# Moving the next batch's image sums, spectra and attention weights forward within layer 0

## The chip, the cores and the metric

The kernel runs on one core of a Trainium2 chip. The metric is the device time of one execution in microseconds (us). Before the change it is 3184.69 us, the median of three runs (3173.39 to 3188.97). Nothing else runs on the chip's other cores.

## The reference

The input `x` has shape (4, 32, 128, 128) in fp32: 4 batches of T = 32 images, each with 128 rows (w) and 128 columns (c). Two layers follow one another, each added to its input.

Layer 0 first normalizes `x` over groups of four columns and then runs an attention among the 32 images of a batch, built from Fourier layers. Cut to what matters here:

```
xa = group_norm(x)                       # per batch
xn = inorm(xa)                           # per image: mean and variance
k, q, v = fno(xn, K), fno(xn, Q), fno(xn, V)     # 32 heads each; k, q at half size
p_attn = softmax(q . k / 64)             # 32 x 32 weights for each head
p = fno(p_attn . v, P)                   # back to one channel
a = inorm(p + xa);  an = inorm(a)
m = gelu(inorm(spectral(an, m0)) + skip)
m = inorm(spectral(m, m1)) + skip
x = x + (inorm(m) + a)
```

`fno` is a spectral convolution (64 x 33 modes of the two-dimensional Fourier transform, with weights) and a scalar skip. Layer 1 is a causal additive attention over 4096 tokens of 128 columns in each batch, and a mixture of eight experts, the best two taken for each token.

## The kernel before

**Layer 1** (from L1022 on) takes some two thirds of the time. It starts when layer 0 ends, apart from a first piece that runs inside layer 0's last batch. The change does not touch it.

**Layer 0** (`layer0`, from L109 on) loops over the 4 batches (L687). The scores of the attention can be formed in Fourier space from spectra of the input images, and so can the values' product; the big tensors k, q and v are never made. One pass of the loop does, in this order of the program:

1. *Value product* (L698 to L788). The image spectra `xd` are read back from DRAM, spread over partitions (`xb`, DMAs of L758, four buffers), copied to PSUM by ScalarE (`xw`, L767), multiplied with the weights `gb` by VectorE (L775) or GpSimd (L773) to `u`, and multiplied with the attention probabilities `pr` on TensorE (L778, `po`). ScalarE puts the sums into `rs` (L788). The skip part `q` is made beside it (`skips`, L719), from `cp`, `cd` and `bd` (L703 to L711).
2. *Value inverse* (L792 to L815). `py` (L798) rearranges `rs` into `yf`; `inverse` (L267) brings each image back in two matmuls (`pv2`, L273, and `four`, L278), and `add_p` (L809) adds it to `q` and takes its statistics (`bn_stats`, L813).
3. *First transform* (L831 to L934). `stats` (L216) gives mean and variance of `q`; `spectra(0, q)` (L852) takes the forward transform: `first_step` (L243) makes `pz`, evacuated to `z1`, and L871 makes `px`; L873 to L891 multiply with the weights (`part1`, `part2`, `spec`) and square. `weighed` (L894) turns the squares into the variance of the result by Parseval's rule: L899, L906, L909, L915, a matmul with ones (`ms`, L314) and a copy (L918). Small operations give the scales `hq`, `hs0` and `hb`.
4. *First per-image inverse* (L935 to L955). `back` (L288) brings the images back in two halves of 16, with matmuls `y1` (L297) and `four` (L308); `gelu` (L939) adds the skip on VectorE (L941), applies the gelu on ScalarE (L944) and takes statistics (L951). `add_attention` (L845) adds the attention part to the input tile (L848), for 16 images after each half.
5. *Next batch's image sums* (L959, `image_sums`, L320). Squares on ScalarE (L326), 16 matmuls that sum rows (L330), small matmuls (`s12`, `mg`, `bg`, `my`) and about 36 small VectorE operations give the group and image statistics, the scaled transform matrix `colg` and the scales `ysc`.
6. *Second transform* (L963 to L967), as the first, of the gelu's result `gl`.
7. *Next batch's image spectra* (L969, `spectra_of_images`, L418). Four groups of 8 images go through `forward` (L253): `pz` (L248), evacuated to `z`, a correction of the mean (L434, L435), `px` in two matmuls for each image (L263, L264), and a scaling to `xx` (L429). Each group's spectra go to DRAM (L445). Then ScalarE copies the lowest modes into `xm` (L457).
8. *Statistics of the second transform* (L970 to L992): `weighed` twice (`v1`, `vc`), two inverse roots (`inv_std`, L204), and the scales `c2`, `c3` and `cq`.
9. *Next batch's attention weights* (L994, `attention_weights`, L487). For each of 17 columns of modes, two products of 128x1024 are made, 22 by VectorE and 12 by GpSimd in all (`pa`, `pb`, L522 and L524, a ring of six buffers), and TensorE multiplies them with weights (`sp`, L528). Then follow the sum `sc`, a softmax (L558 to L564), and a way through DRAM (`prd`, L572, to `pr`, L577).
10. *Second per-image inverse* (L995 to L1016). ScalarE scales `gl` (L999), GpSimd adds it to the input tile `xr` (L1006, 8 images at a time), `back` brings the images back, and VectorE adds them (L1010). The result goes to DRAM as `x1` (L1016).

The program's order is not the order on the chip: a scheduler orders each engine's instructions by readiness in its own model of time and by their place in the program, an earlier place going first. Once the program is built, each engine executes its instructions in the order written. A tile that names a tag shares the buffers of that tag and waits until an older tile there is released. `evacuate` (L184) sends two of three copies out of PSUM to ScalarE and every third to VectorE.

Of the kernel before, what the change touches and what calls it, by code (L numbers as in the profile page):

```python
# [13 lines left out]
P = 128  # L14
# [94 lines left out]
def layer0(  # L109
# [74 lines left out]
    def evacuate(out, in_, sign=1.0):  # L184

        flip[0] = (flip[0] + 1) % 3
        if flip[0]:
            nc.scalar.activation(out, in_, AF.Copy, scale=sign)  # L188
        else:
            nc.vector.tensor_scalar(out, in_, sign, None, ALU.mult)  # L190
# [120 lines left out]
    def sums(name, matrix, src):  # L311

        m = ps.tile(list(src.shape), F32, name=name, tag="wide")
        nc.tensor.matmul(m, matrix, src, start=True, stop=True)  # L314
        return m
# [4 lines left out]
    def image_sums(b, xt):  # L320


        rows8 = ps.tile([64, 4, C], F32, name="rows8", tag="wide")
        for g in GROUPS:
            xx2 = grp.tile([P, GI, C], F32, name="xx2", tag="pr", bufs=6)
            nc.scalar.activation(xx2, xt[:, g : g + GI], AF.Square)  # L326
            for h in range(2):
                m = g // 4 + h
                for k, src in enumerate((xt[:, 4 * m : 4 * m + 4], xx2[:, 4 * h : 4 * h + 4])):
                    nc.tensor.matmul(  # L330
                        rows8[32 * k : 32 * k + 32],
                        one_of_8[:, 7 - m : 39 - m],
                        src,
                        start=m == 0,
                        stop=m == 7,
                    )
        ev = grp.tile([64, 4, C], F32, name="ev", tag="v", bufs=3)
        nc.scalar.copy(ev, rows8)
        s12 = ps.tile([P, 2, 512], F32, name="s12", tag="wide")[:, :, :T]
        for j in range(4):  # L340
            for k in range(2):
                r = slice(32 * k, 32 * k + 8)
                nc.tensor.matmul(s12[:, k, j::4], ev[r, j], ident[r, r], start=True, stop=True)
        sv = small.tile([P, 2, T], F32, name="sv", tag="pk_sq")
        nc.vector.tensor_copy(sv, s12)

        tot = one("tot", 2)
        nc.vector.tensor_reduce(tot, sv, AX.X, ALU.add)
        mg = sums("mg", group, tot)
        gm = one("gm")  # L350
        nc.vector.tensor_copy(gm, mg[:, 0:1])
        gv = one("gv")
        nc.vector.tensor_mul(gv, gm, gm)
        nc.vector.tensor_tensor(gv, mg[:, 1:2], gv, ALU.subtract)
        gr, _ = inv_std("gn_r", gv, 1)
        gs = one("gs")
        nc.vector.tensor_mul(gs, gm, gr)

        both = small.tile([P, 2, 32], F32, name="both", tag="both")
        nc.vector.tensor_scalar(both[:, 0], of_group, gr, None, ALU.mult)  # L360
        nc.vector.tensor_scalar(both[:, 1], of_group, gs, -1.0, ALU.mult, ALU.mult)
        by_group = small.tile([P, 2, 32], F32, name="by_group", tag="by_group")
        nc.vector.tensor_copy(by_group, sums("bg", ones, both))
        n = 1 + 2 * KY
        colg = small.tile([P, 2, n], F32, name="colg", tag="colg")
        nc.vector.tensor_scalar(colg[:, 0], cols1[:, :n], gr, None, ALU.mult)
        nc.vector.tensor_scalar(colg[:, 1], cols2[:, :n], gr, None, ALU.mult)
        m128 = one("m128")
        nc.vector.tensor_scalar(m128, gm, 128.0, None, ALU.mult)

        gs128 = one("gs128")
        nc.vector.tensor_scalar(gs128, gs, 128.0, None, ALU.mult)
        gg = one("gg")
        nc.vector.tensor_mul(gg, gs, gs128)
        gr2 = one("gr2")
        nc.vector.tensor_mul(gr2, gr, gr)
        grs = one("grs")
        nc.vector.tensor_scalar(grs, gs, gr, -2.0, ALU.mult, ALU.mult)
        y12 = small.tile([P, 2, T], F32, name="y12", tag="pk")
        nc.vector.tensor_scalar(y12[:, 0], sv[:, 0], gr, gs128, ALU.mult, ALU.subtract)  # L380
        nc.vector.tensor_scalar(y12[:, 1], sv[:, 1], gr2, gg, ALU.mult, ALU.add)
        nc.vector.scalar_tensor_tensor(
            y12[:, 1], sv[:, 0], grs, y12[:, 1], ALU.mult, ALU.add
        )
        nc.vector.tensor_scalar(y12, y12, 1.0 / NPIX, None, ALU.mult)
        my = sums("my", ones, y12)
        ym, yv = per_image("ym"), per_image("yv")
        nc.vector.tensor_copy(ym, my[:, 0])
        nc.vector.tensor_mul(yv, ym, ym)
        nc.vector.tensor_tensor(yv, my[:, 1], yv, ALU.subtract)  # L390
        yr, _ = inv_std("n1_r", yv)
        ysc = scalars(ALU.mult, "n1_s", yr, par[:, N1W : N1W + 1])
        return by_group, colg, m128, ysc
# [24 lines left out]
    def spectra_of_images(b, xt, normed):  # L418


        _, colg, m128, ysc = normed
        n = 1 + 2 * KY
        xx = modes.tile([P, T, n], F32, name=f"xx_{b}", tag="xx")
        xd = dram.tile([T, 2, KX, KY], F32, name=f"xd_{b}")
        for g in GROUPS:

            def scaled(k, px):
                i = slice(g + k, g + k + 4)
                nc.vector.tensor_tensor(  # L429
                    xx[:, i], px, ysc[:, i].unsqueeze(2).to_broadcast([P, 4, n]), ALU.mult  # L430
                )

            def less_mean(z):
                nc.vector.tensor_scalar(z[:, :, 0], z[:, :, 0], m128, None, ALU.subtract)  # L434
                nc.vector.tensor_scalar(z[:, :, P], z[:, :, P], m128, None, ALU.add)  # L435

            forward([xt[:, g + t] for t in range(GI)], colg[:, 0], colg[:, 1], scaled, less_mean)

            i = slice(g, g + GI)

            for r, y in ((0, 1 + KY), (64, 1)):
                bias = par[r : r + 1, N1B : N1B + 1].to_broadcast([1, GI])
                nc.vector.tensor_copy(xx[r : r + 1, i, y], bias)
            for part in range(2):
                nc.sync.dma_start(  # L445
                    out=xd[i, part].rearrange("t x y -> x t y"),
                    in_=xx[64 * part : 64 * part + 64, i, 1 + KY :],
                )


        nc.vector.tensor_copy(xx[32:33, :, 0], xx[32:33, :, 1 + KY + 32])
        nc.vector.memset(xx[96:97, :, 0], 0.0)


        xm = modes.tile([P, 2 * KA, T], F32, name=f"xm_{b}", tag="xm")
        for k, y0 in enumerate((1 + KY, 1)):
            nc.scalar.copy(  # L457
                xm[:, k * KA : (k + 1) * KA], xx[:, :, y0 : y0 + KA].rearrange("p t y -> p y t")
            )
        return xx, xm, xd  # L460

    def value_weights():
        t1, t2 = (prep.tile([NH, KX, KA], F32, name=f"v{n}", tag=f"t{n}") for n in (1, 2))
# [117 lines left out]

    value_weights()
    normed = image_sums(0, loaded)
    front = spectra_of_images(0, loaded, normed)


    shape = [P, KA, NH]
# [99 lines left out]
    for b in range(B):  # L687
# [105 lines left out]
        for y0 in range(0, KY, 8):  # L793
            n = min(8, KY - y0)
            py = ps.tile([P, 8, 2, T], F32, name="py", tag="b")
            for k in range(n):
                for part in range(2):
                    nc.tensor.matmul(  # L798
                        py[64 * part : 64 * part + 64, k],
                        rs[:, :, y0 + k],  # L800
                        comb[:, 32 * part : 32 * part + 64],
                        start=True,
                        stop=True,
                    )
            evacuate(yf[:, :, :, y0 : y0 + n].rearrange("p t r y -> p y r t"), py[:, :n])
        st = grp.tile([P, T, 6], F32, name="st", tag="st")
        for g in GROUPS:

# [123 lines left out]
        nc.vector.tensor_scalar(hb, hb, par[:, S0 : S0 + 1], None, ALU.mult)  # L932
        nc.vector.tensor_mul(dq, dq, hs0)
        nc.vector.tensor_tensor(hb, hb, dq, ALU.add)  # L934
        gl = big.tile([P, T, C], F32, name=f"g_{b}", tag="y")  # L935
        st = grp.tile([P, T, 6], F32, name="st", tag="st")
        for a in HALVES:
# [14 lines left out]

            back(spec, a, gelu)
            for g in (16 * a, 16 * a + GI):
                add_attention(g)  # L955

        logarithms()
        if b + 1 < B:
            normed = image_sums(b + 1, loaded)  # L959
        else:  # L960
            first((ps, images))

        glm, glv, flat = stats("gl", st)  # L963
# [2 lines left out]
        nc.vector.tensor_copy(dg, d1)  # L966
        spec, sq = spectra(1, gl)  # L967
        if b + 1 < B:
            front = spectra_of_images(b + 1, loaded, normed)  # L969
        v1 = weighed("v1", sq, squares, layers[1][2])  # L970
        vc = weighed("vc", sq, squares, layers[1][3])
        r1, _ = inv_std("r1", v1)
# [17 lines left out]
        nc.vector.tensor_scalar(cq, cq, par[:, MB : MB + 1], None, ALU.add)  # L990
        nc.vector.tensor_mul(dg, dg, c3)
        nc.vector.tensor_tensor(cq, cq, dg, ALU.add)  # L992
        if b + 1 < B:
            weights = attention_weights(b + 1, front)  # L994
        for a in HALVES:  # L995
            groups = [slice(16 * a + g, 16 * a + g + GI) for g in (0, GI)]
            for i in groups:
# [648 lines left out]
```

## Time and profile before

| what | value |
|---|---|
| median of three runs | 3184.69 us (3173.39 to 3188.97) |
| the profiled execution's own time | 3191.62 us |
| its span, first to last instruction | 3189.9 us |
| granted TensorE clock, mean | 0.953 of full |
| busy: TensorE, VectorE, ScalarE, GpSimd | 92%, 72%, 72%, 66% of the span |
| start of py in batches 0 to 3 | 181.6, 440.4, 708.0, 967.5 us |
| layer 0 ends at about | 1105 us |

The span is 1.7 us shorter than the profiled execution's time. In the profile PE is TensorE, PEld its weight loads, DVE VectorE, ACT ScalarE, POOL GpSimd, SP SyncE, whose queue issues most DMAs; ACTq is ScalarE's own issuing of DMAs. An fp32 matmul leaves two records, so that counts of PE instructions in the trace are twice those of the program. In a line of the timeline come the start, the time covered, engine, source line, operation, output<-input with shapes, count, and in brackets the idle time before it and what ended it. Time between two rows that overlap is shared: small operations can start before the one ahead has ended.

### The profile page before, as it was taken

The page shows a single profiled execution, that of the slowest core. Times are in us where ns is not written, and L with a number is a line of the kernel's source. Part 1 is how long each engine was busy: PE and PEld are TensorE (multiplying, and loading weights), DVE is VectorE, ACT ScalarE, POOL GpSimd, SP SyncE. Part 2 cuts the span into 40 slices and gives each one's busy share as a digit, 9 for nine tenths or more (in the row PEclk, how much of TensorE's full clock was granted, in tenths as well). Part 3 has the DMA queues.
Part 4 walks back from the last instruction along what each step waited for, and adds up shares of the span by engine and source line. Part 5 has one row for each costly group of instructions (what it writes and reads, how often), then busy time and mean ns, then how long its engine had stood idle before and what let it go on. Part 6 is the DMA issues. An engine that isn't in the chain of part 4 may idle for free.

```text
span 3189.9 us, 53099 instructions
## 1 busy us (share of the span) xinstructions
PE 2928.7 (92%) x19634; PEld 1438.2 (45%) x19634; DVE 2290.9 (72%) x5035; ACT 2311.7 (72%) x3138; POOL 2102.7 (66%) x1831
## 2 busy tenths in 40 slices
PE   7888798798888789999999999999999999999997
PEld 5366365345546444444344443444444444444443
DVE  5876666667677566777666868866778777687887
ACT  2344243253343589998999999998999999999992
POOL 1621540460451289878788797889878889888773
PEclk6998998899898799999999999999999999999998
DMA  6301310130140211010111010011010011101000
GB/s 140 111 18 30 95 50 3 49 123 1 30 130 2 57 31 31 8 31 7 31 37 24 14 24 14 8 39 31 23 29 9 14 37 24 37 1 31 14 14 14
DMA packets 152308, 112.77 MB, mean 35 GB/s; under 512 B 36878, under 2 KB 140657, under 8 KB 151441
## 3 DMA queue, kind: packets, MB, share of 16 engines
q1 hardware_dynamic: 136209, 103.61, 12.2%
q10 hardware_dynamic: 15840, 5.77, 0.8%
q8 instruction: 155, 2.54, 0.3%
q14 instruction: 104, 0.85, 0.1%
HBM read 68.37 MB, written 20.00 MB: 28 GB/s over the span
## 4 chain that ended last, share of the span: by engine, by line
PE 61%; POOL 12%; ACT 9%; DVE 9%; issue 7%; DMA 1%; ACTq 0%; POOLq 0%; DVEq 0%; SPq 0%
PE d L1446 19%; PE po L1465 11%; PE px L1352 6%; ACT r L1496 4%; PE po L778 4%; PE n L1446 3%; POOL e L1505 3%; POOL e L1504 3%; PE pz L248 2%; PE four L308 2%; ACT e L1512 2%; PE px L871 1%; PE sk L742 1%; POOL kx L1111 1%; DVE r L1501 1%
## 5 line engine op out<-in xcount | busy, mean ns | idle before, releaser
L1501 DVE TENSOR_TENSOR r<-n,r 128x1024 f32<-128x1024 f32 (+1 forms) x1056 | 961.6, 952 | 479.0 <-PE n L1446 389.4
L1504 POOL TENSOR_TENSOR e<-r 128x512 f32<-128x512 f32 x528 | 673.2, 1275 | 268.1 <-DVE r L1501 267.6
L1496 ACT ACTIVATE r<-d 128x1024 f32<-128x1024 f32 (+1 forms) x1056 | 792.9, 802 | 67.4 <-PE n L1446 56.4
L1508 ACT ACTIVATE r<-r 128x1536 f32<-128x1536 f32 x528 | 783.6, 1484 | 16.8
L1505 POOL TENSOR_TENSOR e<-e,r 128x512 f32<-128x512 f32 x528 | 671.3, 1271 | 41.4
L1446 PE MATMUL d<-qe,ke 32*128 32x512 f32 (+3 forms) x2304 | 605.8, 602 | 39.6 <-ACT r L1496 36.5
L1465 PE MATMUL po<-e,kx 128*128 128x512 f32 (+3 forms) x1152 | 594.5, 605 | 15.6 <-POOL e L1517 15.6
L1446 PE MATMUL n<-qe,ke 32*128 32x512 f32 (+3 forms) x2304 | 606.2, 601 | 0.0
L1446 PE MATMUL n<-qf,kf 32*128 32x512 f32 (+3 forms) x2304 | 552.6, 554 | 0.0
L1446 PE MATMUL d<-qf,kf 32*128 32x512 f32 (+3 forms) x2304 | 550.2, 553 | 0.0
L1356 DVE SCALAR_TENSOR_TENSOR xc<-px,wgt,xc 128x128 f32<-128x128 f32 x1024 | 358.1, 350 | 42.2 <-PE px L1352 9.7
L1512 ACT ACTIVATE e<-e 128x512 f32<-128x512 f32 x528 | 325.8, 617 | 66.2 <-POOL e L1505 65.6
L1465 PEld LDWEIGHTS po<-e,kx 128*128 128x128 f32 x1152 | 175.5, 188 | 392.8 <-issue 306.9
L1446 PEld LDWEIGHTS d<-qe,ke 32*128 32x128 f32 x2304 | 176.5, 183 | 359.3 <-ACT r L1496 339.5
L773 POOL TENSOR_TENSOR u<-xb,gb 128x858 f32<-128x858 f32 (+1 forms) x120 | 233.1, 1968 | 139.5 <-PE po L778 128.0
L1446 PEld LDWEIGHTS d<-qf,kf 32*128 32x128 f32 x2304 | 220.2, 186 | 176.1 <-issue 163.8
L1352 PE MATMUL px<-we,x2t 128*128 128x512 f32 x512 | 264.0, 601 | 6.8 <-DVE xc L1356 6.0
L775 DVE TENSOR_TENSOR u<-xw,gb 128x858 f32<-128x858 f32 (+1 forms) x200 | 206.6, 1082 | 59.2 <-PE po L778 46.6
L885 POOL TENSOR_TENSOR spec<-part,part 128x512 f32<-128x512 f32 x16 | 24.8, 1550 | 333.4 <-ACT z L188 75.2
L1446 PEld LDWEIGHTS n<-qf,kf 32*128 32x128 f32 x2304 | 228.3, 185 | 19.2 <-issue 11.4
L778 PE MATMUL po<-u,pr 128*32 128x429 f32 (+1 forms) x1280 | 191.1, 548 | 26.8 <-DVE u L775 11.7
L524 POOL TENSOR_TENSOR pb<-xm 128x1024 f32<-128x1024 f32 x48 | 90.7, 1913 | 159.1 <-ACT xm L457 152.8
(388 smaller groups left out, 3953.9 us busy)
## 6 DMA issues: line engine op xcount, KB each, us to landing
xb<-xd SPq DMA_DIRECT2D x128, 214.5 KB
xc<-x SPq DMA_DIRECT2D x29, 512.0 KB
x<-x SPq DMA_DIRECT2D x16, 512.0 KB
qf<-qe SPq DMA_DIRECT2D x64, 128.0 KB
out<-xc SPq DMA_DIRECT2D x15, 512.0 KB
xb<-xd SPq DMA_DIRECT2D x32, 198.0 KB
gb<-gd SPq DMA_DIRECT2D x4, 1056.0 KB
x<-in_x SPq DMA_DIRECT2D x8, 512.0 KB
```

The lines of the kernel that those rows point to most:

```text
L773: nc.gpsimd.tensor_tensor(u, xb, gk, ALU.mult)
L778: nc.tensor.matmul(po[32 * j : 32 * j + 32], pr[:, i, k], u[:, r], start=i == 0 and k == 0, stop=i == 3 and k == 1,)
L1352: nc.tensor.matmul(px, x2t[:, k * P : (k + 1) * P], we[:, e0 : e0 + 4], start=True, stop=True)
L1356: nc.vector.scalar_tensor_tensor(xc[:, k], px[:, e], wgt[:, k, e0 + e : e0 + e + 1], xc[:, k], ALU.mult, ALU.add)
L1446: nc.tensor.matmul(o, k, q, start=turn == 0 or g > 0, stop=turn == 1 or g > 0)
L1465: nc.tensor.matmul(sums[c, h][:, q0 : q0 + c1 - c0], kx[:, jb], e[:, c0:c1], start=jb == 0, stop=is_last and q0 > 2 * P, skip_group_check= ...
L1496: nc.scalar.activation(r[:, g], d, AF.Ln, scale=1.0 / DSCALE)
L1501: nc.vector.tensor_tensor(r[:, g], part, r[:, g], ALU.mult)
L1504: nc.gpsimd.tensor_tensor(e, r[:, 1], r[:, 2], ALU.add)
L1505: nc.gpsimd.tensor_tensor(e, e, r[:, 0], ALU.add)
L1508: nc.scalar.activation(r, r, AF.Exp, scale=-1.0)
L1512: nc.scalar.activation(e, e, AF.Exp)
```

## The change

The sums, spectra and weights of the next batch stay what they are and move to other places in the program:

- The image sums go from behind the gelu stage to between `py` and the value inverse (into step 2).
- The spectra become a generator. Its first yield hands out the tiles `xx`, `xm` and `xd`; each of the four groups of images is then one step. One step is taken ahead of the first per-image inverse, and one ahead of each group of 8 images of `add_attention`, so that two come between the two halves and the last one after the second half (into step 4). The fourth step runs to the end, with the copies to `xm`.
- The attention weights go from behind the statistics of the second transform to just behind `spectra(1, gl)`, ahead of `v1` and `vc` (between steps 6 and 8).
- `sv` gets a buffer of its own, where it shared one with `pk_sq` of `stats`; `y12`, which shared one with `pk`, is dropped, its operations being done in place on `sv`.

```diff
@@ image_sums
-        sv = small.tile([P, 2, T], F32, name="sv", tag="pk_sq")
+        sv = small.tile([P, 2, T], F32, name="sv", tag="sv")
...
-        y12 = small.tile([P, 2, T], F32, name="y12", tag="pk")
-        nc.vector.tensor_scalar(y12[:, 0], sv[:, 0], gr, gs128, ALU.mult, ALU.subtract)
-        nc.vector.tensor_scalar(y12[:, 1], sv[:, 1], gr2, gg, ALU.mult, ALU.add)
-        nc.vector.scalar_tensor_tensor(
-            y12[:, 1], sv[:, 0], grs, y12[:, 1], ALU.mult, ALU.add
-        )
-        nc.vector.tensor_scalar(y12, y12, 1.0 / NPIX, None, ALU.mult)
-        my = sums("my", ones, y12)
+        nc.vector.tensor_scalar(sv[:, 1], sv[:, 1], gr2, gg, ALU.mult, ALU.add)
+        nc.vector.scalar_tensor_tensor(sv[:, 1], sv[:, 0], grs, sv[:, 1], ALU.mult, ALU.add)
+        nc.vector.tensor_scalar(sv[:, 0], sv[:, 0], gr, gs128, ALU.mult, ALU.subtract)
+        nc.vector.tensor_scalar(sv, sv, 1.0 / NPIX, None, ALU.mult)
+        my = sums("my", ones, sv)
@@ spectra_of_images
         xd = dram.tile([T, 2, KX, KY], F32, name=f"xd_{b}")
+        xm = modes.tile([P, 2 * KA, T], F32, name=f"xm_{b}", tag="xm")
+        yield xx, xm, xd
         for g in GROUPS:
...
+            if g + GI < T:
+                yield
...
-        xm = modes.tile([P, 2 * KA, T], F32, name=f"xm_{b}", tag="xm")
...
-        return xx, xm, xd
@@ before the loop over batches
-    front = spectra_of_images(0, loaded, normed)
+    front, *_ = spectra_of_images(0, loaded, normed)
@@ behind py, ahead of the value inverse
+        if b + 1 < B:
+            normed = image_sums(b + 1, loaded)
         st = grp.tile([P, T, 6], F32, name="st", tag="st")
@@ ahead of the first per-image inverse
+        ahead = iter(())
+        if b + 1 < B:
+            ahead = spectra_of_images(b + 1, loaded, normed)
+            front = next(ahead)
+            next(ahead)
         gl = big.tile([P, T, C], F32, name=f"g_{b}", tag="y")
...
             back(spec, a, gelu)
             for g in (16 * a, 16 * a + GI):
+                next(ahead, None)
                 add_attention(g)

         logarithms()
-        if b + 1 < B:
-            normed = image_sums(b + 1, loaded)
-        else:
+        if b + 1 == B:
             first((ps, images))
...
         spec, sq = spectra(1, gl)
         if b + 1 < B:
-            front = spectra_of_images(b + 1, loaded, normed)
+            weights = attention_weights(b + 1, front)
         v1 = weighed("v1", sq, squares, layers[1][2])
...
         nc.vector.tensor_tensor(cq, cq, dg, ALU.add)
-        if b + 1 < B:
-            weights = attention_weights(b + 1, front)
         for a in HALVES:
```

## The prediction

> **What bounds the kernel now.** Layer 0 takes about 1105 of the span's 3189.9 us; the change stays inside its batches 0, 1 and 2, each of which prepares the next. I cut batch 0 into stages by events in the timeline (py starts, statistics of q, first gelu add, last gelu statistics, end of the second transform, sod, last product, next po) and asked for the busy time of each stage. Columns: stretch, its length, then busy time (instructions) of PE, PEld, DVE, ACT, POOL, then granted clock, DMA share, GB/s:
>
> ```profile
> 181.60:208.60 27.00, 25.55 (x290) 24.37 (x294) 15.10 (x46) 9.46 (x12) 0.00 (x0) 1.00 0.01 2
> 208.60:235.70 27.10, 20.35 (x219) 14.79 (x209) 23.27 (x88) 6.77 (x17) 3.44 (x2) 0.79 0.01 2
> 235.70:257.10 21.40, 19.47 (x114) 7.08 (x114) 16.71 (x66) 16.47 (x37) 0.00 (x0) 0.94 0.00 1
> 257.10:276.80 19.70, 19.58 (x191) 13.95 (x190) 10.00 (x53) 6.83 (x15) 1.26 (x1) 1.00 0.01 1
> 276.80:308.80 32.00, 28.38 (x232) 27.25 (x226) 20.40 (x72) 8.30 (x18) 1.26 (x1) 0.86 0.24 57
> 308.80:342.20 33.40, 24.31 (x130) 4.88 (x130) 26.85 (x23) 13.12 (x35) 31.73 (x16) 0.78 0.06 16
> 342.20:371.50 29.30, 20.44 (x165) 9.48 (x166) 17.37 (x46) 6.42 (x12) 4.17 (x3) 1.00 0.32 80
> ```
>
> Call them A (py, inverse), B (first transform, its statistics), C (gelu), D (image sums, second transform), E (image spectra), F (attention products), G (softmax, last inverse). In A and E the PE is the full engine. In B VectorE is: the PE timeline shows the hole.
>
> ```profile
> 220.50 1.74 PE L871 MATMUL px<-z,cst 128*32 128x256 f32 x24
> 228.57 0.63 PE L314 MATMUL ms<-v_s,ones 128*128 128x32 f32 x2 [6.34 <-DVE v_s L915]
> 229.13 4.14 PE L297 MATMUL y<-cst,spec 32*128 32x128 f32 x64
> ```
>
> F is bound by POOL, 31.7 of 33.4 us, which does more than products: the POOL timeline has the four adds of L1006 among them.
>
> ```profile
> 309.04 3.78 POOL L524 TENSOR_TENSOR pb<-xm 128x1024 f32<-128x1024 f32 x2 [28.68 <-ACT xm L457]
> 312.77 2.37 POOL L1006 TENSOR_TENSOR x<-x,g 128x1024 f32<-128x1024 f32 x1
> 315.83 2.37 POOL L1006 TENSOR_TENSOR x<-x,g 128x1024 f32<-128x1024 f32 x1 [0.69 <-ACT g L999]
> 318.15 3.79 POOL L524 TENSOR_TENSOR pb<-xm 128x1024 f32<-128x1024 f32 x2
> ```
>
> The scalings that feed these adds run under the products on ScalarE, and G ends on VectorE, where the cp reductions and the next batch's first u stand behind the last adds of L1010:
>
> ```profile
> 309.88 12.04 ACT L999 ACTIVATE g<-g,cq,c 128x128 f32<-128x128 f32 x31
> ...
> 365.29 2.16 DVE L1010 SCALAR_TENSOR_TENSOR x<-four,c,x 128x128 f32<-128x128 f32 x8 [0.25 <-PE four L308]
> 367.36 1.28 DVE L705 TENSOR_TENSOR cd<-cm,sel 128x512 f32<-128x512 f32 x2
> 368.56 1.91 DVE L706 TENSOR_REDUCE cp<-cd 128x16 f32<-128x512 f32 x2
> 370.38 1.04 DVE L775 TENSOR_TENSOR u<-xw,gb 128x858 f32<-128x858 f32 x1
> ```
>
> **What the Trainium skill says.** "TensorE: Matmul & The Clock Gate" (Part 1, the HAM clock gate) says an idle window of about 3.4 us halves the PE's clock. The trace agrees at the hole in B: after 6.34 us idle the clock is 0.50 until 235. It also halves after idles of only 1.5 us in E (0.50 from 300 to 315), so I can't promise a warm clock in C. The same page (opening table, queue depth) calls ScalarE, VectorE and GpSimd strict FIFO. The trace agrees: products of L524 wait behind L1006. This decides G below. "GPSIMD Engine Reference" (1. Specifications) says POOL shares its SBUF interface with VectorE instructions that have two SBUF inputs. In batch 1, L899 took 1.91 instead of 1.21 us beside L885; the durations I use contain such meetings already.
>
> **The change part by part.** From the instruction order of the built program, by stage; times are gains (-) or losses (+) per batch, for batch 0 first.
>
> A, image sums added. PE gets 16 matmuls of L330; x and xx run in pairs, 0.43 us per record pair, two of these per pair of matmuls. Three precede py, 13 follow it: 6.5 x 0.86 = 5.6 us, of which 1 us fills the wait for yf. The 36 small VectorE operations of the sums (0.13 to 0.2 us each) fall in a stretch where VectorE is full (in batch 1, 8 adds at 0.6, 32 statistics at 0.22 and three evacuations at 0.6 take 13.5 of the 14.5 us from the first q add on): about 30 x 0.13 = 3.9 us. The first q add comes 5.5 us later (rows, s12, mg), hence 5.5 + 3.9, less 0.7 of slack: **+8.7** (bounds +6, +11). Squares (L326) run before this already. The x loads they need are issued a whole batch earlier and land under the value products.
>
> B, group 0 of the spectra added. PE work (8 pz at 0.255, 16 px at 0.223: 5.6 us) lies in the hole and costs nothing; were the hole gone, it would be +5.6. VectorE, which bounds B, gets 2 evacuations (0.6), 2 mean corrections (0.2), 2 scalings (0.44) and 2 copies: **+3.1**.
>
> C, groups 1 and 2 added, between the two halves of the inverse. Half one: 16 adds at 0.26 and 16 statistics at 0.22, behind gelus at 0.39 with a table load of 1.3: 9 us. Then in PE's order the rest of y1 (3.1), 32 px (7.1), 10 pz (2.5) and their evacuations stand before half two's first inverse matmul; this starts about 19 us after the first add, and needs 8.6. Together 27.8 against 21.4: **+6.4**. With a half clock px takes 0.43: +7 more, the upper bound; the lower one is +3. In batch 1, C took 27.6 at a clock of 0.64: there +0.2.
>
> D loses the image sums and rows' tail, and gets group 3: px 3.6, then the second transform, whose evacuations on ScalarE now wait for xm (2.25) and a table load (1.3). I count 17.3 us against 19.7, 21.7 and 21.4: **-2.4**, -4.4, -4.1 (bounds +4, -6).
>
> E goes but for sod's matmuls, 1.3 us: **-30.7**, -30.1, -31.3. The xd writes (8 issues of 0.65 us on SP) and the xb loads behind them move ahead with it; SP is idle there, and po waits for VectorE's u, not for xb, so this gains nothing.
>
> F: POOL's order has the 12 products and then the four adds: 12 x 1.91 = 22.9 us. VectorE becomes the bound: sod 1.2 and 22 products, issued every 1.15 us, 26.5; PE at a half clock would need 17 x 1.7 = 29. I take 28: **-5.4**.
>
> G pays for it. VectorE's order puts v1 and vc of the second transform (L899, L906, about 1.2 us each, four) *behind* the 22 products, since the weights now come first, and all that follows from them is late: r1, rm, c2, cq, then 32 scalings on ScalarE, four adds on POOL, the last adds on VectorE. From the last product on: four reductions and softmax to 10.3 us; about 25 small operations and two inverse roots of 1.7 to cq at 15.1. The pr DMA, queued on ScalarE before the scalings, waits for prd until about 14.5, so it is not later. 16 scalings at 0.39 end at 21.4, the second add of 2.37 at 23.8; half two's 16 with three evacuations end at 29.3, its last add at 31.7. Then 12 last adds (3.3), an evacuation, cd, 4 adds (3.1), cp (1.9), u (1.0): po starts at 41 against 29.3, 30.6 and 27.3: **+11.7**, +10.4, +13.7. Bounds: +6 if the last adds overlap more, +18 if nothing does.
>
> Sums: -8.6 in batch 0, -17.6 in batch 1, -9.0 in batch 2, together -35.2. Batch 3 and layer 1 get the same instructions as before. The new sv tag takes the place of two shared ones; it ends no wait that the trace shows. The profiled execution took 3191.6 us, 1.7 more than its span and 0.2% over the median of 3184.7; the same step from the median gives **3150**.
>
> **Rivals.**
> 1. *As above*, 3112 to 3172, about 3150. For it: E is a stretch of 32 us with PE full, whose work fits into stages where PE or the other engines have room. Against: it must survive seven terms.
> 2. *Tail decides*: G's chain costs the full +18, and A the full +11; then a batch gains about 3 and the kernel takes about 3175 to 3185, near no change. For it: every link is on another in-order queue.
> 3. *Slower*: the spectra stand in series in C. PE executes in order, so half two of the gelu stage waits for 32 px matmuls whose evacuations stand behind the gelus on ScalarE. If nothing overlaps and the clock is half there, C takes 21.4 plus 32 px at 0.43 (13.8) and three rounds of evacuation, correction and scaling (about 2.5 each): +21 instead of +6.4, so that a batch loses about 3 on average and the time is about 3195 to 3205. It decides once C passes 40 us. Against: the gelu stage in batches 0 and 2 leaves ScalarE 5 and VectorE 5 us idle.
> 4. *More than thought*: the filled hole keeps the clock, C costs +2, and F runs at 26.5: 5 to 6 us more per batch, about 3132. That the change does nothing (the scheduler having hoisted this work already) is excluded: in the order before, sums and spectra stand behind the gelus.
>
> **Chances.** First 0.60, fourth 0.14, second 0.15, third 0.11. The range that leaves out 2 in 10 reaches from 3112 to 3186. A measurement of this kernel can tell about 0.5%, 16 us. Faster by more: cases one and four but for their edge, 0.74; within it: 0.15; slower: 0.11.
>
> **What would show it.** After: py to first q statistics about 36 us; no stretch like E; POOL's L1006 adds behind all twelve products; last product to next po about 41 us with ScalarE's scalings in it. Wrong if that last stretch stays near 30, or grows beyond 47, if C passes 40, or if F stays at 33 without the adds.

## The result, and the profile after

| | us |
|---|---|
| the changed kernel, median of 12 runs | 3197.9 (3186.0 to 3208.0) |
| the kernel before, 12 runs beside it | 3177.7 (3173.4 to 3189.0) |
| ratio, 95% interval | 1.0053 (1.0035 to 1.0072) |
| forecast | 3150 (3112 to 3186) |

The change makes the kernel slower by half a per cent, some 17 to 20 us, where I forecast 35 us faster. The profiled execution took 3204.4 us, its span 3202.7, at a mean clock of 0.948 (before: 0.953); it is 6.5 us above the median of the twelve. One execution of `e7_vahead` below, 4013.5 us at a mean clock of 0.66, is left out of that run's ratio.

The time is lost in the place that the prediction named, batches 0 to 2 of layer 0: from the first py to that of batch 3 it was 786 us and is 801. A second profile of each kernel (`before_again` and `after_again`, below) has 770 and 798. All stages below are cut as in the prediction. First batch 0 of the changed kernel, A to G, with the columns of before (length, then TensorE, its weight loads, VectorE, ScalarE, GpSimd, clock):

```profile
180.80:219.90 39.10, 37.02 (x336) 30.63 (x338) 19.30 (x80) 10.65 (x17) 0.00 (x0) 0.91 0.01 1
219.90:253.80 33.90, 27.03 (x291) 21.54 (x284) 24.95 (x98) 10.41 (x25) 3.46 (x2) 0.94 0.07 18
253.80:283.00 29.20, 27.12 (x202) 21.57 (x202) 21.92 (x82) 17.62 (x41) 0.00 (x0) 0.96 0.18 41
283.00:297.50 14.50, 14.34 (x188) 12.17 (x188) 6.33 (x26) 7.21 (x12) 1.27 (x1) 1.00 0.15 41
297.50:299.40 1.90, 0.88 (x18) 0.77 (x13) 1.21 (x2) 0.60 (x1) 0.00 (x0) 1.00 0.00 0
299.40:326.10 26.70, 24.16 (x130) 5.04 (x130) 26.20 (x25) 0.42 (x1) 23.34 (x13) 0.87 0.00 1
326.10:367.30 41.20, 23.08 (x170) 10.61 (x166) 27.64 (x83) 19.51 (x48) 13.87 (x7) 0.81 0.22 57
```

Row five is E: 32 us have become 1.9. Rows one to three, A to C, have taken most of it back (12.1, 6.8 and 7.8 us); in A and C TensorE is nearly full, in B it is not (27.0 of 33.9 us). The last row, G, took more than F gave. Counted from py to py, batch 0 gains 2.6 us, and batches 1 and 2 lose about 9 each. There D and G look different; this is batch 2:

```profile
811.20:837.00 25.80, 24.88 (x218) 21.67 (x218) 6.79 (x28) 8.87 (x15) 1.27 (x1) 0.77 0.09 24
...
865.50:912.80 47.30, 33.68 (x171) 15.89 (x167) 28.36 (x84) 19.09 (x47) 13.84 (x7) 0.66 0.19 49
```

Not many more matmuls than in batch 0 (218 records instead of 188 in D, 171 instead of 170 in G) keep TensorE busy for 24.9 us instead of 14.3 and for 33.7 instead of 23.1, at clocks of 0.77 and 0.66. The TensorE timeline shows where D's half clock begins: ahead of it TensorE waits 4.3 us for an evacuation `z` that stands behind the gelus on ScalarE, and then the image spectra's px run, each row of two records 0.43 us after the last one, where in batch 0 it is 0.22.

```profile
806.06 1.10 PE L308 MATMUL four<-v,cst 128*128 128x512 f32 x2 [0.52 <-DVE g L947]
811.46 0.80 PE L248 MATMUL pz<-cst,g 128*128 128x128 f32 x2 [4.30 <-ACT z L188]
812.05 0.53 PE L263 MATMUL px<-colg,z 128*128 128x67 f32 x2
812.38 0.64 PE L264 MATMUL px<-colg,z 128*128 128x67 f32 x2
812.80 0.63 PE L263 MATMUL px<-colg,z 128*128 128x67 f32 x2
```

The hole of B, batch 0 again, on TensorE: px now lies around ms, at full clock, and y1 (L297) starts as soon as they end. But the next matmul waits 5.2 us for VectorE.

```profile
240.59 0.36 PE L314 MATMUL ms<-v_s,ones 128*128 128x32 f32 x2
...
243.49 0.39 PE L264 MATMUL px<-colg,z 128*128 128x67 f32 x2
243.81 2.07 PE L297 MATMUL y<-cst,spec 32*128 32x128 f32 x64
245.81 0.71 PE L248 MATMUL pz<-cst,x 128*128 128x128 f32 x4
251.69 2.07 PE L308 MATMUL four<-v,cst 128*128 128x512 f32 x2 [5.18 <-DVE v L190]
```

VectorE's timeline says why. It waited in order for px, twice (L428). The adds of the attention part (L849), with which it filled such times before, come later: 15 of them, 4 us, stand ahead of the evacuation of y1.

```profile
242.13 0.44 DVE L428 TENSOR_TENSOR xx<-px,n_s 128x268 f32<-128x268 f32 x1 [0.72 <-PE px L264]
...
243.91 0.44 DVE L428 TENSOR_TENSOR xx<-px,n_s 128x268 f32<-128x268 f32 x1 [0.77 <-PE px L264]
...
246.91 4.02 DVE L849 SCALAR_TENSOR_TENSOR x<-q,ra,x 128x128 f32<-128x128 f32 x15
...
250.95 0.69 DVE L190 TENSOR_SCALAR v<-y 128x512 f32<-128x512 f32 x1
```

In the kernel before four were left there, 1.1 us:

```profile
233.74 1.13 DVE L848 SCALAR_TENSOR_TENSOR x<-q,ra,x 128x128 f32<-128x128 f32 x4
```

In batch 1 the hole is there as well, 4.7 us, and px come behind it at half clock, 16 in 6.9 us between ms (494.1) and y1 (501.4).

F and G on GpSimd and ScalarE: GpSimd's adds stand behind all its products and wait 18.8 us for the scalings, which follow cq on ScalarE. The evacuations of y1 (L188) stand behind these.

```profile
322.84 3.78 POOL L523 TENSOR_TENSOR pb<-xm 128x1024 f32<-128x1024 f32 x2 [0.74 <-DVE pa L521]
345.39 2.34 POOL L1009 TENSOR_TENSOR x<-x,g 128x1024 f32<-128x1024 f32 x1 [18.77 <-ACT g L1002]
```

```profile
342.13 6.26 ACT L1002 ACTIVATE g<-g,cq,c 128x128 f32<-128x128 f32 x16 [2.81 <-DMA pr<-prd]
348.30 1.06 ACT L188 ACTIVATE v<-y 128x512 f32<-128x512 f32 x2
```

That is the tail as forecast: cq came 16.0 us after the end of the last product (15.1 worked out), po 41.2 after it (41).

### The profile page after: what moved, and what is told of

It is laid out like the page before. It is cut to its first block, busy times and chain, and to the rows that moved or that the text cites. A ratio compares the mean times of both kernels' runs of the same rounds, so it can differ in the third digit from the quotient of the medians.

```text
span 3202.7 us, 53092 instructions
## 1 busy us (share of the span) xinstructions
PE 2937.5 (92%) x19634; PEld 1453.0 (45%) x19634; DVE 2282.9 (71%) x5035; ACT 2309.1 (72%) x3138; POOL 2103.3 (66%) x1831
## 3 DMA queue, kind: packets, MB, share of 16 engines
q1 hardware_dynamic: 136209, 103.61, 12.2%
## 4 chain that ended last, share of the span: by engine, by line
PE 61%; POOL 11%; ACT 10%; DVE 9%; issue 7%; DMA 2%; SPq 0%; POOLq 0%; DVEq 0%; ACTq 0%
PE d L1449 18%; PE po L1468 10%; PE px L1355 6%; ACT r L1499 4%; PE po L777 4%; PE n L1449 3%; POOL e L1508 3%; POOL e L1507 3%; PE pz L248 2%; PE four L308 2%; ACT e L1515 2%; PE sk L741 1%; DVE r L1504 1%; POOL kx L1114 1%; PE px L872 1%
## 5 line engine op out<-in xcount | busy, mean ns | idle before, releaser
L1468 PE MATMUL po<-e,kx 128*128 128x512 f32 (+3 forms) x1152 | 594.3, 605 | 17.3 <-POOL e L1520 17.3
L1359 DVE SCALAR_TENSOR_TENSOR xc<-px,wgt,xc 128x128 f32<-128x128 f32 x1024 | 358.2, 350 | 42.7 <-PE px L1355 10.6
L886 POOL TENSOR_TENSOR spec<-part,part 128x512 f32<-128x512 f32 x16 | 24.8, 1552 | 409.2 <-DVE part L883 190.8
L1449 PEld LDWEIGHTS n<-qf,kf 32*128 32x128 f32 x2304 | 228.0, 185 | 18.7 <-issue 11.2
L777 PE MATMUL po<-u,pr 128*32 128x429 f32 (+1 forms) x1280 | 194.2, 549 | 24.8 <-DVE u L774 14.4
L1449 PEld LDWEIGHTS n<-qe,ke 32*128 32x128 f32 x2304 | 177.8, 183 | 9.5 <-DVE r L1504 1.2
```

What stands on the lines that cost most here:

```text
L777: nc.tensor.matmul(po[32 * j : 32 * j + 32], pr[:, i, k], u[:, r], start=i == 0 and k == 0, stop=i == 3 and k == 1,)
L1359: nc.vector.scalar_tensor_tensor(xc[:, k], px[:, e], wgt[:, k, e0 + e : e0 + e + 1], xc[:, k], ALU.mult, ALU.add)
L1449: nc.tensor.matmul(o, k, q, start=turn == 0 or g > 0, stop=turn == 1 or g > 0)
L1468: nc.tensor.matmul(sums[c, h][:, q0 : q0 + c1 - c0], kx[:, jb], e[:, c0:c1], start=jb == 0, stop=is_last and q0 > 2 * P, skip_group_check= ...
```

## The experiments

A filler below is a matmul into a tile that nothing reads. Ratios are to the kernel before, run on the same chip, with their 95% intervals.

**The three moves one by one.** `e1_sums` moves the image sums alone:

```diff
+        if b + 1 < B:
+            normed = image_sums(b + 1, loaded)
         st = grp.tile([P, T, 6], F32, name="st", tag="st")
...
-            normed = image_sums(b + 1, loaded)
```

> Image sums alone are moved to the value inverse; spectra and weights stay where the kernel before has them. If the three moves simply add up, A grows by 10 to 12 us in each of the batches 0 to 2, as in the changed kernel, D falls by 5 to 7 (the sums' matmuls and small VectorE operations leave it), E, F and G stay at 31, 33 and 29: +4 to +7 per batch, 12 to 21 us slower than before. If the sums lay hidden under the second transform, D stays at 19 to 22 and the kernel is some 30 us slower. If A's growth belongs to something else, A stays at 27 and the kernel is 15 us faster.

Measured: 1.0027 (1.0015 to 1.0038), 9 us slower. A grew by 10.6, 12.9 and 9.6 us, as expected; D fell by 12.4, 12.0 and 5.2 against the first profile, more than I thought, so that the loss is a little below the 12 to 21 us of the expectation. A's growth is the sums' own.

`e2_weights` moves the weights alone:

```diff
             front = spectra_of_images(b + 1, loaded, normed)
+            weights = attention_weights(b + 1, front)
         v1 = weighed("v1", sq, squares, layers[1][2])
...
-            weights = attention_weights(b + 1, front)
         for a in HALVES:
```

> Attention weights alone are moved ahead of v1 and vc; image sums and spectra stay where the kernel before has them. If the tail is the weights' own doing (v1, cq, 32 scalings and four adds all stand behind the products), F falls to 26 and G grows to 42 to 44 as in the changed kernel: +7 to +8 per batch, some 20 to 25 us slower than before. If G's excess over the predicted 41 comes from the clock that the moved spectra leave behind, G is 37 to 40 here, and the kernel is 5 to 12 us slower.

Measured: 1.0006 (0.9994 to 1.0017), no difference. F fell to 26.7, 26.7 and 26.4, G grew to 37.8, 39.8 and 38.7. G has the size of the second theory, but the kernel isn't 5 to 12 us slower. The run keeps the new buffer of `sv` too, which by this run costs nothing that can be seen. F and G of batch 0:

```profile
308.10:334.80 26.70, 24.38 (x130) 4.62 (x130) 26.23 (x23) 0.79 (x3) 22.16 (x12) 0.84 0.06 19
334.80:372.60 37.80, 21.66 (x173) 9.69 (x170) 21.94 (x75) 19.51 (x48) 13.82 (x7) 0.85 0.24 62
```

So F's gain comes back in G by the weights alone, and G lacks 3.4 us (batch 0) of what it has in the changed kernel. There VectorE is busy 27.6 us in G, here 21.9: with the spectra still in E, the reductions of v1 and vc run beside them (at 281 and 287 us), and the scalings start 12.5 us after the last product, not 16.0.

`e3_spectra` moves sums and spectra and leaves the weights behind cq:

```diff
-            weights = attention_weights(b + 1, front)
         v1 = weighed("v1", sq, squares, layers[1][2])
...
         nc.vector.tensor_tensor(cq, cq, dg, ALU.add)
+        if b + 1 < B:
+            weights = attention_weights(b + 1, front)
```

> Image sums and spectra are moved as in the changed kernel, the weights stay behind cq as in the kernel before. If the moves add up, A to E are those of the changed kernel (A +11, B +6.5, C +8, D +1, E -30 per batch: about -3.5), and F and G those of before (33 and 29): some 10 us faster than before. If the weights' early start is what the removal of E needs, F or G is longer than before and the kernel is level with before or slower.

Measured: 1.0235 (1.0216 to 1.0253), 75 us slower. The moves do not add up. E, F and G of batch 0:

```profile
299.70:313.80 14.10, 3.52 (x36) 3.12 (x36) 11.73 (x23) 1.97 (x6) 5.91 (x3) 0.63 0.00 0
313.80:349.40 35.60, 25.11 (x126) 4.57 (x126) 34.12 (x39) 12.25 (x33) 19.87 (x11) 0.86 0.00 0
349.40:390.10 40.70, 30.22 (x166) 12.92 (x166) 17.51 (x46) 7.07 (x14) 12.20 (x6) 0.69 0.22 57
```

The first row is what lay beside the image spectra in E: the work from v1 on towards cq, 12 us of VectorE with TensorE idle for 10.6 of 14.1 us; the rest of that chain stands in F, which is at 35.6 us again. In the kernel before this work lies under the spectra. With the spectra gone it stands alone, and the last inverse has a clock of 0.69. So the weights' move is no gain of its own (`e2_weights`), but without it the spectra's move is far dearer.

`e7_vahead` asks whether the chain can be had earlier in the changed kernel:

```diff
-        if b + 1 < B:
-            weights = attention_weights(b + 1, front)
         v1 = weighed("v1", sq, squares, layers[1][2])
         vc = weighed("vc", sq, squares, layers[1][3])
+        if b + 1 < B:
+            weights = attention_weights(b + 1, front)
```

> The changed kernel with v1 and vc of the second transform weighed ahead of the attention weights, so that VectorE's four 1.2 us operations and the first inverse root stand ahead of the 22 products. If the tail's length is the chain from v1 to cq, G falls by 6 to 8 us and E grows by no more than 3: 10 to 15 us faster than the changed kernel. If no other work lies beside that chain once the image spectra are gone from there, E grows by what G loses (8 to 9, TensorE and GpSimd idle meanwhile): level with the changed kernel or up to 10 us slower.

Measured: 1.0083 (1.0055 to 1.0112), above the changed kernel's 1.0053, with overlapping intervals. In batch 0, E grew from 1.9 to 14.1, and G fell from 41.2 to 35.2. In this profile the chain costs more in front than behind.

**The place of the spectra.** `e5_early` takes group 0 ahead of v0, so that its px precede ms:

```diff
         spec, sq = spectra(0, q)
+        ahead = iter(())
+        if b + 1 < B:
+            ahead = spectra_of_images(b + 1, loaded, normed)
+            front = next(ahead)
+            next(ahead)
         v0 = weighed("v0", sq, squares, layers[0][2])
...
-        ahead = iter(())
-        if b + 1 < B:
-            ahead = spectra_of_images(b + 1, loaded, normed)
-            front = next(ahead)
-            next(ahead)
         gl = big.tile([P, T, C], F32, name=f"g_{b}", tag="y")
```

> The changed kernel with group 0 of the image spectra emitted right behind the first transform's spectra, ahead of v0: its px matmuls then stand ahead of ms and lie in TensorE's hole, not between ms and y1. Theory one, TensorE's work is conserved and only an idle stretch that is filled gains: the 4 to 5 us idle ahead of ms shrink, B falls from 33.8 to 28 to 30 in every batch, the other stages stay: 12 to 18 us faster than the changed kernel, level with before or up to 3 us faster. Theory two, VectorE is B's bound and group 0's evacuations now delay v0 by the 3 us that they cost: B stays at 33, no gain.

Measured: 1.0056 (1.0034 to 1.0077), level with the changed kernel. B fell by 3 us in batches 1 and 2, but not in batch 0, where px ran at half clock and VectorE waited for it:

```profile
222.80:259.10 36.30, 30.82 (x293) 25.37 (x286) 25.86 (x99) 10.54 (x25) 2.54 (x2) 0.86 0.07 17
481.20:511.90 30.70, 26.84 (x292) 21.47 (x290) 25.18 (x99) 8.97 (x24) 2.54 (x2) 1.00 0.08 20
737.30:768.20 30.90, 24.93 (x290) 20.55 (x289) 25.87 (x100) 11.55 (x26) 2.53 (x2) 0.99 0.07 20
```

`e6_behind` takes every group one step later:

```diff
             front = next(ahead)
-            next(ahead)
...
                 next(ahead, None)
                 add_attention(g)
+        for _ in ahead:
+            pass
```

> The changed kernel with every group of the image spectra one step later: none ahead of the first inverse half, groups 0 and 1 behind the first half, 2 and 3 behind the second. Theory one, TensorE's work is conserved: B falls to 27 (-6.5), C stays as it is, D grows by the 5.6 to 7 us of one group, the kernel is level with the changed one within 0.3%. Theory two, it was the place ahead of y1 that cost, since all of the gelu stage waits for it, while behind the second half it lies beside the gelus and z waits: D grows by 2 to 3 only, 10 us or more faster than the changed kernel.

Measured: 1.0099 (1.0076 to 1.0123), some 15 us slower than the changed kernel. B fell by 3 to 6 only, C took 32.5, 32.5 and 33.5 us, and D 31.0, 24.8 and 31.5. Neither theory's sizes hold. No place tried for the groups was better than the change's own.

**The clock.** `e4_warm` fills the hole ahead of ms:

```diff
         spec, sq = spectra(0, q)
+        for _ in range(3):
+            for h in range(2):
+                warm = ps.tile([P, 512], F32, name="warm", tag="wide")
+                nc.tensor.matmul(
+                    warm,
+                    ident,
+                    sq[:, 0, 4 * h : 4 * h + 4].rearrange("p a b -> p (a b)"),
+                    start=True,
+                    stop=True,
+                )
```

> The changed kernel with six matmuls more per batch behind the first transform's spectra (128x512, into a tile that nothing reads), about 0.85 us each at full clock, to fill the hole of TensorE ahead of ms. If the half clock is what made B, C and D longer than I predicted, the clock in these stages of batches 1 and 2 goes from 0.73 to 0.85 to over 0.95, B falls by 2 to 4, C of batch 1 to about 30, D of batches 1 and 2 to about 15 as in batch 0: 10 to 15 us per batch, 20 to 30 us faster than the changed kernel. If the order of the work is what costs (px ahead of y1, z behind the gelus), the filler changes the clock but not the stages: level with the changed kernel, or up to 5 us per batch slower.

Measured: 1.0069 (1.0046 to 1.0091), level with the changed kernel. B's clock rose to 1.00 in batches 0 and 1, and B fell to 30.0 and 30.1, just the +3 that I had forecast for it. But batch 0 shows that this isn't the clock alone, for there it was 0.94 in the changed kernel too: the fillers also changed the order, and VectorE has seven adds left ahead of the evacuation of y1 instead of 15. D of batch 1 fell from 25 to 19.5 at a clock of 0.96, as forecast in kind, but C of batch 2 went the other way, from 25.8 to 39.6 at a clock of 0.74.

`e9_warmtail` puts five fillers (128x512) behind sc:

```diff
+        for _ in range(5):
+            warm = ps.tile([P, 512], F32, name="warm", tag="wide")
+            nc.tensor.matmul(
+                warm, ident, spt.rearrange("p t s -> p (t s)"), start=True, stop=True
+            )
         ph = grp.tile(nn, F32, name="ph", tag="pr", bufs=6)
```

> The changed kernel with five matmuls more per batch behind sc (128x512, into a tile that nothing reads; 0.85 us each at full clock), in the 3 to 4 us in which TensorE waits for vc_s, ahead of the last inverse. If the half clock is what makes G 42 to 48 instead of the 38 to 40 that the weights alone gave (e2_weights), the clock of G goes from 0.67 to 0.82 to over 0.9 and G falls by 3 in batches 0 and 1 and by 8 in batch 2: some 14 us faster than the changed kernel. If the scalings in ScalarE's queue ahead of the evacuations of y1 set G's end, the clock rises and G stays, or grows by 1 to 2 per batch.

Measured: 1.0051 (1.0033 to 1.0070), level with the changed kernel. G is 44.4, 45.1 and 41.8 us (changed kernel: 41.2, 43.2, 47.3): where the clock rose far, in batch 2 from 0.66 to 0.91, G fell by 5.5; in batches 0 and 1, where it only came to 0.83 and 0.82, G grew by 2 to 3.

`e12_warmd` puts eight (128x256) in the wait at the end of the gelu stage:

```diff
             for g in (16 * a, 16 * a + GI):
+                if a and g == 16 and b + 1 < B:
+                    for _ in range(8):
+                        warm = ps.tile([P, 512], F32, name="warm", tag="wide")
+                        nc.tensor.matmul(
+                            warm[:, :256],
+                            ident,
+                            gl[:, 22:24].rearrange("p t c -> p (t c)"),
+                            start=True,
+                            stop=True,
+                        )
                 next(ahead, None)
```

> The changed kernel with eight matmuls more per batch (128x256, half at most of 0.86 us each at full clock, into a tile that nothing reads) behind the last four of the gelu stage, in the 4.3 us in which TensorE waits for z behind the gelus (batch 2). If the half clock in D comes from that idle stretch ahead of group 3's px, the clock of D rises from 0.70 to 0.78 to over 0.9 in batches 1 and 2 and D falls from 26 to 18 or less in both; batch 0, where D is at full clock, stays or grows by up to 3: 10 to 16 us faster than the changed kernel. If the stream of px itself lets the clock fall, D stays at 25 and the kernel is level or up to 3 us per batch slower.

Measured: 1.0075 (1.0052 to 1.0098), level with the changed kernel. D's clock rose to 0.97 in batch 1 and px ran at full clock there. TensorE in batch 1:

```profile
549.24 1.85 PE L248 MATMUL pz<-cst,g 128*128 128x128 f32 x8 [1.68 <-ACT z L188]
550.89 4.63 PE L964 MATMUL warm<-g,ident 128*128 128x256 f32 x16
555.36 0.33 PE L263 MATMUL px<-colg,z 128*128 128x67 f32 x2
555.53 0.39 PE L264 MATMUL px<-colg,z 128*128 128x67 f32 x2
555.75 0.39 PE L263 MATMUL px<-colg,z 128*128 128x67 f32 x2
```

So in D the half clock isn't a property of px: filled ahead of them, the same px run twice as fast. But the fillers took 4.6 us here and 6.8 in batch 2, about what the clock gave: D is 24.1 and 28.5 us, and 19.3 in batch 0, which had been warm. My estimate of their price, half of 0.86 us each, held only at full clock.

`e13_allwarm` has the fillers of all three:

> The fillers of e4_warm, e9_warmtail and e12_warmd together in the changed kernel (6, 5 and 8 matmuls per batch that nothing reads, some 13 us of TensorE at full clock, all behind waits). If the half clock is all that stands between the changed kernel and a gain, the stages fall to what batch 0 showed at full clock or below, 39, 30, 28, 15, 2, 26 and 40 us, 180 in all for A to G against the 189 to 191 of the second profile of before: 15 to 25 us faster than before. If TensorE's work is the bound and its idle time only changes place, the clock is high, A to G stay at 187 to 192 per batch, and the kernel is level with before.

Measured: 1.0101 (1.0078 to 1.0124), some 15 us slower than the changed kernel and worse than either expectation. A to G took 187.0, 199.9 and 205.9 us, 592.8 in all; the changed kernel's two profiles have 591.9 and 592.0. The clock was 1.00 in B of all batches and 0.88 or more in D, its mean over A to G 0.91 (changed kernel 0.85, kernel before 0.88 and 0.90), and nothing was won. TensorE's idle time fell from 100 to 81 us and its busy time rose from 491 to 512. All warm it was not: C of batches 1 and 2 had clocks of 0.83 and 0.74, and C of batch 2 took 38.8 us instead of 25.8.

**The noise of one profile.** Both kernels once more:

> The changed kernel once more, for a second profile. If the half clock in D of batches 1 and 2 and in G of batch 2 belongs to the order of the program, the clock is low in the same stages again: D 25 and 26 us, G of batch 2 48 us. If it belongs to the execution, they fall to 14 to 20 and 42.

> The kernel before once more, for a second profile. If C of batch 1 (27.6 us at a clock of 0.63 in the first profile) belongs to the execution, it is 19 to 21 here, as in batches 0 and 2 and in e2_weights; A, B, D, E, F and G of all three batches stay within 1 us of the first profile.

Measured: the changed kernel took 3204.0 us, with D at 14.5, 25.9 and 25.8 and G of batch 2 at 47.2: the half clock is in the same stages, which speaks for the program's order as its source. Both profiles lie above the median of twelve, so how the faster executions look is not shown. The kernel before took 3173.3 us, C of batch 1 was 19.1 instead of 27.7, and no other stage of a batch moved by over 3 us (I had expected 1): that half clock came with the one execution that I had worked from.

**A part worth having.** The one gain of the weights' move was that GpSimd's adds left the products' stage. `f1_vadd` does half of that in the kernel before, and moves nothing else:

```diff
-                nc.gpsimd.tensor_tensor(xr[:, i], xr[:, i], gl[:, i], ALU.add)
+                eng = nc.vector if a else nc.gpsimd
+                eng.tensor_tensor(xr[:, i], xr[:, i], gl[:, i], ALU.add)
```

> The kernel before with one edit: the two adds of the second half (L1006) go to VectorE, where they stand behind the last product and ahead of the softmax maximum, which waits for sc there anyway. If F is bound by GpSimd (31.7 of 33.4 us) and G's start by TensorE's sc, F falls by the two adds, 2 x 2.37 us, to 28 to 29, until VectorE (26.9 us) is the bound, and G stays within 1 us: -4 per batch, 10 to 14 us faster than before. If what F loses comes back in G, as with the weights alone (e2_weights: -7 and +9), the kernel is level with before.

Measured: 3172.1 against 3179.3 us, ratio 0.9986 (0.9975 to 0.9997): some 4 to 7 us faster where 10 to 14 were expected, and barely clear of the noise, but the fastest of the kernels here. F fell to 29.2, 29.9 and 29.2 us, and G is 29.6, 32.5 and 27.5. F and G of batch 0, and VectorE at their border:

```profile
312.10:341.30 29.20, 23.86 (x130) 4.45 (x130) 26.44 (x24) 13.15 (x35) 26.79 (x14) 0.87 0.06 18
341.30:370.90 29.60, 20.71 (x163) 9.46 (x164) 21.85 (x49) 6.42 (x12) 5.42 (x3) 1.00 0.32 80
```

```profile
341.22 4.58 DVE L1007 TENSOR_TENSOR x<-x,g 128x1024 f32<-128x1024 f32 x2
346.58 0.68 DVE L558 TENSOR_REDUCE mx<-sc 64x16 f32<-64x512 f32 x1 [0.78 <-PE sc L547]
```

The adds fit ahead of the maximum, which still waits 0.8 us for sc.

## Why the prediction was wrong

Sums over batches 0 to 2, us; measured is the mean of two profiles of each kernel:

| stage | before | after | change | forecast | off by |
|---|---|---|---|---|---|
| A | 80.5 | 114.6 | +34.1 | +26.1 | +8.0 |
| B | 82.4 | 102.5 | +20.1 | +9.3 | +10.8 |
| C | 65.5 | 91.9 | +26.4 | +13.0 | +13.4 |
| D | 62.8 | 65.7 | +2.9 | -10.9 | +13.8 |
| E | 93.7 | 5.7 | -88.0 | -92.1 | +4.1 |
| F | 99.5 | 80.1 | -19.4 | -16.2 | -3.2 |
| G | 88.6 | 131.6 | +43.0 | +35.8 | +7.2 |
| sum | 573.0 | 592.1 | +19.1 | -35.0 | +54.1 |

1. **The sum of A to E asked for more than there was.** In batch 0 before, these five stages last 127.2 us, and TensorE is busy in them for 113.3 (the rows that I showed). My terms for them add up to -14.9 us, all of the 13.9 us of idle time and more, though the matmuls only changed place and I counted no gain of clock. I moved 28 us of TensorE work, mostly into A to D, in which it was already busy for 85 of 95 us, and priced it by what each engine's queue added, never by TensorE's total. A to E did get shorter in batch 0, from 127.2 to 118.6 us, but their idle time fell only from 13.9 to 12.2: the other 6.9 us are busy time, at a higher clock (B and E had 0.79 and 0.86 before). Over A to G and three batches the two profiles of before have TensorE busy for 484 and 474 us and idle for 95 and 93; those of after 491 and 492, and 100 each. So the idle time was not filled: it left F (9 to 2.5 us in batch 0) and came up in G (9 to 18). Of the 19 us lost, about 13 are busy time, at a mean clock of 0.85 instead of 0.88 and 0.90, and about 6 are idle time.

2. **B, +3.1 forecast, +6.7 measured: "lies in the hole and costs nothing" failed.** The px did lie in the hole in batch 0, but VectorE, which bounds B, waited for them in order, and its adds were pushed behind hb and ahead of the evacuation of y1. In batch 1 the hole stayed and px followed it at half clock. I had priced VectorE's added work and not its added waits: in batch 0 it is busy for 1.7 us more in B and idle for 5.1 us more. My reading of the clock there was short, too: it fell at 224.5, 2.3 us into the wait, and was back at 238.2, not at 235.

3. **C and D, 27 us of the error: the clock, for which I had made no place in the likeliest case.** I wrote that I couldn't promise a warm clock in C, and kept it for the upper bound; for D I took 17.3 us at full clock in all batches. Batch 0 has 14.5, batches 1 and 2 have 25 to 26 at 0.70 to 0.77, in two profiles alike. Where another order left the clock high, D of batch 1 took less: 18.7 us at 1.00 in `e5_early`, 19.5 at 0.96 in `e4_warm`. So about 6 us of it go with the clock. C of batch 1 is a second error: its forecast of +0.2 started from 27.6 us at half clock in one execution. Without that, 19.1 to 34.9 or 39.0. C never passed 40, yet the kernel became slower: my third rival had the mechanism (work in series at half clock), but looked for it in C alone, where it is spread over B, C, D and G.

4. **A, +8.7 forecast, +11.4 measured, and G, +11.9 and +14.3.** Right in kind. A is at its upper bound, and alone it is the same (`e1_sums`). In G the chain through cq, the scalings and the adds runs as I counted it, and batches 0 and 1 are within about 2 us of it; the rest is batch 2 at a clock of 0.66, of which `e9_warmtail` took 5.5 us away.

5. **E and F, right.** The spectra left E to within 1.4 us a batch, F became VectorE's at 26.7 us (I took 28). That F would pay and G be paid, and that both come from the place of v1 in VectorE's queue, held, and `e2_weights` shows that this part is worth nothing. `e3_spectra` shows what it avoids.

The full clock alone would not have made the forecast true: batch 0 ran its first five stages at 0.91 or more, and gained 2.6 us, not 8.6. The twelve executions agree. Four of them had a mean clock of 0.953 to 0.955 and took 3186.0 to 3190.4 us; 17 executions of the kernel before at these clocks, beside the experiments, took 3177.5 to 3190.7, their median 3184.8. At an equal clock the two kernels are thus some 4 us apart: most of the 20 us lost go with the clock, but none of the 35 us expected come back with it. That they go together does not say which causes which; `e13_allwarm` raised the clock and won nothing. What the changed kernel would take at full clock throughout stays open, since every filler that raised the clock took about as much of TensorE as it gave.

## What to carry to other kernels

Before pricing a move engine by engine, add up the busy time of the fullest engine over all stages that give and take: a move can win only the idle time that it really fills and what a higher clock takes off the busy time, and a forecast that needs all of the idle time should not be believed. A stage that goes takes its cover with it: ask what ran beside it for nothing. And take one execution's clock for what it is: profile twice before a stage at half clock becomes the base of a difference, and count every wait of TensorE that a new order brings ahead of matmuls.

## What was not expected of the hardware

- **Short waits were enough to halve the clock, and some streams got it back sooner than others.** The Trainium skill ("TensorE: Matmul & The Clock Gate", Part 1) gives an idle window of about 3.4 us before the clock halves, and as much busy time to get it back. In batch 1 of the changed kernel the clock fell behind two waits of 1.7 and 0.7 us at the end of C: in the last 3.41 us ahead of the fall (543.05 to 546.46) TensorE was busy for 1.68 us. In batch 2 it fell 2.1 us into the wait of 4.3 us, and was busy for 1.10 of the last 3.41. So no wait had to be as long as the window; an idle share of half was enough here. Once the wait in batch 2 had ended, px and what followed stayed at half clock from 811.5 to 822.9, 11.4 us without a gap. With the 128x256 fillers there, the full clock was back 3.7 us after the wait in batch 1 and 6.2 in batch 2. Whether it was the 67 columns or the window's phase was not tried.
- **An add moved from GpSimd to VectorE was no faster there.** The two adds of L1007 took 2.29 us each on VectorE in batch 0 of `f1_vadd`, against 2.36 on GpSimd, while L899, of the same shape and also with two SBUF inputs, takes 1.21 with GpSimd at rest. GpSimd worked on u meanwhile, and that took 3.00 instead of 2.00 us. This agrees with the interface that GpSimd shares with VectorE for instructions of two SBUF inputs ("GPSIMD Engine Reference", 1. Specifications), and it is where the missing 3 to 7 us of `f1_vadd`'s forecast may be.
